# Reordered edges of a two-layer graph kernel: the weights' product, the first two pairs of scores, the last sums and the first block of layer 1

## The chip, the cores and the metric

The kernel runs on one NeuronCore of a Trainium2 chip. The metric is the device time of one execution in microseconds, as the median of several runs. The core has five engines that run side by side, each in its own program order: PE (TensorE, matrix products and transposes into the eight banks of PSUM), DVE (VectorE), ACT (ScalarE), POOL (GpSimd) and SP (SyncE, which here only issues DMAs). They wait for each other through semaphores.

## The reference

`x` is 4096 x 512 and `adj` 4096 x 4096 (mostly zeros). Two layers follow each other, each with a residual:

```python
# layer 0: attention with a dense bias
h = relu(layernorm(x))
q, k, v = h @ Wq.T + bq, h @ Wk.T + bk, h @ Wv.T + bv
a = q @ k.T / sqrt(512) + adj + adj
x = x + softmax(a) @ v
# layer 1: graph attention, 8 heads of 64
h = relu(layernorm(x))
nX = (h @ W) per head, standardized over its 64 values
kg = leaky_relu(at1 + at2.T, 0.2) * adj          # at1, at2: nX times a1, a2
x = x + elu(softmax(where(adj != 0, kg, -32768)) @ nX + nX)
```

## The kernel before

Rows are taken in 32 blocks of 128, eight superblocks ("sb") of four blocks, and eight chunks ("ic") of 512 query rows. Every helper call passes through `seq`, which keeps instructions in the order in which they are written, so the code's order is each engine's order.

**Weights.** The two weight matrices Wq and Wk are multiplied once, so that scores are h A h' with A = Wq' Wk. Each 128-row block of Wq and Wk is loaded (line 584, alternating), turned by four PE transposes into a bank and copied out by ACT (Wq) or DVE (Wk) (`turn_weights`, 590 to 594). After all eight come 16 products of 128 x 512 (line 607) with the contraction index in the outer loop and four banks `pa` open at once, and ACT moves the banks to `a_sb` (616).

**Projection.** For each superblock, `hidden(sb)` turns the normalized rows (PE 445, ACT relu 446) and POOL makes four sums `hS` of their blocks (454 to 457). `values_of(sb)` and `queries(sb)` are products in a form with seven instead of eight block products (`seven`, 491 to 517): four stages, PE products into banks Z and X, DVE additions out of them (512, 522, 556), and after each stage one function of the list `between`. `weight_sums` makes POOL's sums of the weights (470 to 473). The first superblocks have an order of their own: values 0, hidden 1, values 1, queries 0, hidden 2, queries 1; from superblock 2 on it is values, hidden of the next, queries. Stores of `qs`, `ts` to `q_d` (574) go through SP.

**Attention of layer 0.** A "pair" is two blocks of 128 keys against a chunk of 512 queries; 8 x 16 pairs, numbered by s = 0, 2, ..., 254. `stage(s, n)` for n = 0 to 3 makes the scores of a pair (line 724) in two halves of the bank `xz`, and DVE adds each part onto the turned block of `adj` (736); ACT takes the exponent (740). POOL makes the sums `S` of the pair (`pair_sums`, 752 to 764), and `weighted(s, ...)` adds the pair's seven products with the values to the banks M1 to M7 (779). In the main loop (891) `weighted(s)` and `stage(s + 2)` alternate. Before the loop, the stages of pair 0 run alone (880 to 882), and between them DVE turns the blocks 2 and 3 of `adj` (`swap`, 341) and prepares their masks for layer 1 (`for_layer_1`, 714 and 716, stored by SP at 717 and 718). DVE turns blocks 0 and 1 inside the last `queries` (681).

**Ends of chunks.** `chunk_end` (814) combines M1 to M7 into the output rows in pieces that `end()` issues. For the last chunk, `total_of_rows` (860) lets PE sum POOL's `total` over the partitions (867) before `weighted(254, (3, .), (6, .))`, and the last additions read bank M6 on DVE (835).

**Layer 1's projection.** A new set of pools is opened, among them a new PSUM pool over the same banks. `turn(r)` (1272) transposes the normalized block r (1275), ACT takes the relu (1276), `project(r)` multiplies it with W (1285), and `variance`, `deviation`, `standardize` follow. Block 0 is turned first, then block 1, then block 0 is projected. The main loop of layer 1 (512 steps, 1493) follows and isn't touched.

## Time and profile before

| | us |
|---|---|
| runs of the kernel: 3552.49, 3554.74, 3554.75 | median 3554.74 |
| the execution that was profiled | 3555.78 |
| its span in the profile | 3553.7 |
| PE busy | 3500.3 (98%) |
| DVE busy | 2572.2 (72%) |
| POOL busy | 2284.5 (64%) |
| ACT busy | 1770.7 (50%) |

The span is the time from the first to the last instruction of the profile; 2.1 us of the profiled execution lie outside of it. "Busy" counts a PE instruction from its start to its modelled end. An fp32 product of 128 x 128 by 256 columns is recorded as two matmul instructions. The program has three parts: the projection of layer 0 until 236 us, its attention until 1803 us, layer 1 from then on.

### The profile page before, as it was taken

Reading aid. Unit: us, or ns where it says so; the run is one execution under the profiler, and the core shown is the slowest. Engines: PE = TensorE matmul, PEld = TensorE weight load, DVE = VectorE, ACT = ScalarE, POOL = GpSimd, SP = SyncE. Lnnn points to the kernel's source line nnn. Section 1 sums busy time; section 2 is a strip of 40 time slices with the busy share of each in tenths; the row PEclk is TensorE's granted clock in tenths of the full one; section 3 lists DMA queues with packets and bytes.
Section 4 is the critical chain, followed back from the end, with each engine's and each line's share of the span. In section 5 each row is a group of like instructions: output and inputs, shape, how many; then the busy total and the mean of one; then the engine's idle time right before and its main releaser. Section 6 shows DMA issues by size and latency. Waiting matters only on the chain.

```text
span 3553.7 us, 59795 instructions
## 1 busy us (share of the span) xinstructions
PE 3500.3 (98%) x21898; PEld 2153.7 (61%) x21898; DVE 2572.2 (72%) x4256; ACT 1770.7 (50%) x1578; POOL 2284.5 (64%) x1863
## 2 busy tenths in 40 slices
PE   9999999999999999999999999999999999999998
PEld 7888888888888888888877222222322223222222
DVE  6765565656566666656557888888888888888887
ACT  2100111111111111111133899999999999999997
POOL 6754444444445444444556788888888888888886
PEclk9999999999999999999999999999999999999999
DMA  6678788888888888888758777777787777777775
GB/s 215 218 245 232 227 243 247 237 244 241 243 241 243 237 249 237 239 251 231 230 127 174 208 206 201 211 209 210 214 220 208 215 211 206 200 212 209 214 211 149
DMA packets 633358, 778.81 MB, mean 219 GB/s; under 512 B 78496, under 2 KB 461152, under 8 KB 623840
## 3 DMA queue, kind: packets, MB, share of 16 engines
q1 hardware_dynamic: 615344, 741.81, 72.4%
q0 software_dynamic: 16464, 31.98, 5.2%
q8 instruction: 174, 2.85, 0.3%
q10 hardware_dynamic: 1248, 1.11, 0.1%
q14 instruction: 128, 1.05, 0.1%
HBM read 592.71 MB, written 174.19 MB: 216 GB/s over the span
## 4 chain that ended last, share of the span: by engine, by line
PE 90%; DVE 7%; ACT 1%; DMA 1%; issue 1%; POOL 0%; SPq 0%; DVEq 0%; ACTq 0%; POOLq 0%
PE accs L1092 25%; PE XZ L724 21%; PE M L779 21%; PE r L1053 4%; PE r L1023 4%; PE l L1033 3%; PE X L505 3%; PE l L1053 3%; PE Z L505 2%; DVE t L1080 2%; PE y L1285 1%; PE pt L1156 1%; DVE x L835 1%; DVE y L1169 1%; PE accs L1285 1%
## 5 line engine op out<-in xcount | busy, mean ns | idle before, releaser
L1077 POOL TENSOR_TENSOR t<-t,g 128x1024 f32<-128x1024 f32 x512 | 1224.7, 2400 | 273.0 <-DVE t L1071 237.1
L1092 PE MATMUL accs<-t,nX 128*64 128x512 f32 x4096 | 1002.9, 605 | 4.7 <-DVE ob L1146 4.7
L1084 ACT ACTIVATE t<-t 128x2048 f32<-128x2048 f32 (+1 forms) x527 | 976.5, 1853 | 0.2 <-POOL t L1077 0.2
L1071 DVE SCALAR_TENSOR_TENSOR t<-u,at2m,r 128x512 f32<-128x512 f32 x1024 | 719.2, 744 | 193.6 <-issue 152.1
L740 ACT ACTIVATE aT<-aT 128x512 f32<-128x512 f32 x256 | 161.2, 630 | 1393.1 <-DVE aT L736 1393.1
L736 DVE TENSOR_TENSOR aT<-aT,XZ 128x256 f32<-128x256 f32 x891 | 351.5, 418 | 581.0 <-PE XZ L724 576.6
L1080 DVE TENSOR_TENSOR t<-l,g 128x1024 f32<-128x1024 f32 x512 | 623.6, 1218 | 0.0
L1039 ACT ACTIVATE l<-l 128x1024 f32<-128x1024 f32 x512 | 516.3, 1008 | 117.2 <-PE l L1033 66.0
L1092 PEld LDWEIGHTS accs<-t,nX 128*64 128x64 f32 x4096 | 246.5, 136 | 462.3 <-issue 449.6
L724 PE MATMUL XZ<-qt,hS 128*128 128x256 f32 x2040 | 483.0, 379 | 1.0
L752 POOL TENSOR_TENSOR S<-aT 128x256 f32<-128x256 f32 x128 | 93.2, 728 | 511.7 <-ACT aT L740 507.3
L724 PEld LDWEIGHTS XZ<-qt,hS 128*128 128x128 f32 x2040 | 386.8, 190 | 56.4 <-DVE aT L736 4.2
L724 PE MATMUL XZ<-qt,hT 128*128 128x256 f32 x1532 | 374.0, 380 | 3.7 <-DVE aT L736 3.7
L764 POOL TENSOR_TENSOR total<-total,aT 128x256 f32<-128x256 f32 x360 | 324.1, 914 | 9.4
L724 PEld LDWEIGHTS XZ<-qt,hT 128*128 128x128 f32 x1532 | 292.0, 191 | 44.1 <-DVE aT L736 4.1
L1023 PEld LDWEIGHTS <-z 6*128 6x128 bf16 x2048 | 52.4, 91 | 422.3 <-DVE t L1071 354.6
L753 POOL TENSOR_TENSOR aT<-aT 128x256 f32<-128x256 f32 x128 | 93.2, 728 | 285.7 <-ACT aT L740 285.7
L779 PE MATMUL M<-v,aT 128*128 128x256 f32 x1024 | 263.7, 380 | 0.0
L779 PE MATMUL M<-tv,aT 128*128 128x256 f32 x1024 | 262.6, 379 | 0.0
L779 PE MATMUL M<-v,S 128*128 128x256 f32 x1024 | 243.7, 381 | 0.0
L716 DVE SCALAR_TENSOR_TENSOR gs<-ng,aT 128x512 f32<-128x512 bf16 x254 | 224.5, 884 | 8.7
L779 PEld LDWEIGHTS M<-v,aT 128*128 128x128 f32 x1024 | 195.1, 191 | 26.7
(256 smaller groups left out, 4537.7 us busy)
## 6 DMA issues: line engine op xcount, KB each, us to landing
g<-gT_d SPq DMA_DIRECT2D x128, 1024.0 KB
ag<-in_adj_dram SPq DMA_DIRECT2D x256, 256.0 KB
hS<-s_d SPq DMA_DIRECT2D x64, 1024.0 KB
gT_d<-gs SPq DMA_DIRECT2D x256, 256.0 KB
nb<-nT_d SPq DMA_DIRECT2D x128, 512.0 KB
nx<-nT_d SPq DMA_DIRECT2D x256, 256.0 KB
hT<-h_d SPq DMA_DIRECT2D x64, 768.0 KB
tv<-vt_d SPq DMA_DIRECT2D x128, 384.0 KB
```

Source lines behind the costliest of these rows:

```text
L716: seq(nc.vector.scalar_tensor_tensor(gs, ng, G_MASKED / NEG_BIG, aT, ALU.mult, ALU.add))
L724: seq(nc.tensor.matmul(out, a, b, start=start and k == 0, stop=k == 1, skip_group_check=not start,))
L736: seq(nc.vector.tensor_add(p, before, part))
L764: seq(nc.gpsimd.tensor_add(t, t, a))
L779: seq(nc.tensor.matmul(sums[ic][i][:, u, :], a[:, ts(u, P)], b, start=jt == 0 and u == 0, stop=jt == NB - 2, skip_group_check=u == 1,))
L1039: seq(nc.scalar.activation(lefts[n], lefts[n], AF.Relu, scale=4.0))
L1053: seq(nc.tensor.matmul(out[first + 2 * r][ts(c, HD), :], ident_b[rows, rows], masks[r != c][rows, jt % JB, :], start=False, stop=True, ski ...
L1071: seq(nc.vector.scalar_tensor_tensor(t[:, 2 + e, :], u4[:, e, :], at2m[:, jt, h : h + 1], right[e], ALU.max, ALU.add))
L1077: seq(nc.gpsimd.tensor_mul(t[:, 2:4, :], t[:, 2:4, :], both_heads(n)))
L1080: seq(nc.vector.tensor_mul(logits[n][:, 0:2, :], lefts.pop(n), both_heads(n)))
L1084: seq(nc.scalar.activation(t, t, AF.Exp))
L1092: seq(nc.tensor.matmul(accs[ts(e, HD), hf, :], nX[jt // SB][:, jt % SB, hg * HG + 2 * hf + e, :], t[:, hf + 2 * e, :], start=jt == 0, stop ...
```

## The change

- The loads of Wk come before those of Wq. PE turns the four blocks of Wk and two of Wq, then makes the product for one output block (four products into one bank), turns the third block of Wq, makes the next output block, and so on; ACT and DVE take turns at the copies. `stats(0)`, `roots(0)`, `scale(0)` stand between the third and the fourth output block. bq is loaded by SP ahead of the second superblock of x, no longer by ACT.
- All superblocks run in the order values, hidden of the next, queries. The bias of the keys (`c_sb`) is made in four parts between the stages of values 0, the attention vectors between those of values 1; the loads of W move behind the load of superblock 3. `qs` is always the one buffer of its pool. `first_turned` takes the place of the buffer `prod`.
- DVE turns four blocks of `adj` inside the last `queries`. Before the main loop the stages of pairs 0 and 2 alternate, each pair with banks of its own; the masks of blocks 0 to 3 come later, one in each of four passes of the loop. The first pass has no scores to make, and its `weighted` has another order.
- In the last chunk the sums of M6 are copied by ACT to `of_6`, from which DVE adds them. `total_of_rows` of the last chunk comes after the last products, and its result is copied to SBUF by DVE. Block 0 of layer 1 is loaded in the last chunk (`load_first`) and turned in its last pass (`turn_first`) through the bank `xz` into `first_turned`; layer 1's loop turns block 1 before it projects block 0.

```diff
-            for k in range(KC):
-                for name, w in (("q", wqT), ("k", wkT)):
+            for name, w in (("k", wkT), ("q", wqT)):
+                for k in range(KC):
                     seq(nc.sync.dma_start(out=raw[name][:, k, :], in_=w[ts(k, P), :]))
...
+            seq(nc.sync.dma_start(out=bq_sb, in_=bq[None, :].to_broadcast([P, D])))
             xts[1] = load_x(1)
...
             for k in range(KC):
-                turn_weights("q", k, nc.scalar.copy)
-                turn_weights("k", k, nc.vector.tensor_copy)
-            for c in range(SB):
-                for k in range(KC):
+                turn_weights("k", k, nc.vector.tensor_copy if k % 2 else nc.scalar.copy)
+            for k in range(2):
+                turn_weights("q", k, nc.vector.tensor_copy if k % 2 else nc.scalar.copy)
+            for k in range(KC):
+                pa = psum.tile([P, 512], F32, name="pa", tag="XZ"[k % 2], bufs=2)
+                for c in range(SB):
                     seq(nc.tensor.matmul(
-                        pa[k], turned["q"][:, c, ts(k, P)], turned["k"][:, c, :],
+                        pa, turned["q"][:, c, ts(k, P)], turned["k"][:, c, :],
                         start=c == 0, stop=c == SB - 1,
                     ))
-            stats(0, *range(SB))
-            roots(0)
-            scale(0)
+                if k + 2 < KC:
+                    turn_weights("q", k + 2, nc.scalar.copy)
+                elif k + 1 < KC:
+                    stats(0, *range(SB))
+                    roots(0)
+                    scale(0)
+                seq(nc.scalar.activation(a_sb[:, k, :], pa, AF.Identity, scale=half_scale))
             stats(1, *range(SB))
...
             hidden(0, xts.pop(0))
+            wa = weight_sums(a_sb, [t.rearrange("p (k c) -> p k c", k=2) for t in ats])
             scale(1)
...
+            def key_bias(k):
+                w = wk_rows[:, k, :]
+                seq(nc.vector.tensor_mul(w, w, bq_sb))
+                seq(nc.vector.tensor_reduce(c_sb[:, k : k + 1], w, AX.X, ALU.add))
+                if k + 1 == KC:
+                    seq(nc.vector.tensor_scalar_mul(c_sb, c_sb, half_scale))
...
-            queries(0, [lambda: next(vectors, None)] * 4)
-            hidden(2, xts.pop(2))
-            queries(1, ahead_of(3))
-            for sb in range(2, NS):
+            for sb in range(NS):
                 if sb + 2 < NS:
                     xts[sb + 2] = load_x(sb + 2)
...
-                    firsts = [t.rearrange("p h e -> p (h e)") for t in aa]
+                    firsts = [t.rearrange("p h e -> p (h e)") for t in aa] + [bv_sb, ats[0]]
                     queries(sb, [
-                        lambda s=s: turn_blocks(firsts[s], raws.pop(s), s) for s in range(2)
+                        lambda s=s: turn_blocks(firsts[s], raws.pop(s), s) for s in range(SB)
                     ])
...
-            w = {"alone": psum.tile([P, 2, H], F32, name="z0", tag="M3", bufs=1)[:, 0]}
-            for n, (f, s) in enumerate(((swap, 2), (for_layer_1, 2), (swap, 3), (for_layer_1, 3))):
-                stage(0, n, w)
-                f(s)
+            both = [
+                (0, {"alone": True, "z": bank_of(3), "x": bank_of(6)}),
+                (2, {"alone": True, "z": bank_of(5), "x": xz[:, 1]}),
+            ]
+            for n in range(4):
+                for s, w in both:
+                    stage(s, n, w)
+            w = {}
             pair_sums(0)
-            for s in range(2):
+            pair_sums(2)
+            for s in range(4):
                 later.setdefault(2 * s, []).append(lambda s=s: for_layer_1(s))
...
-                more, ahead = s + 2 < n_tiles, s + 4 < n_tiles
+                more, ahead = 0 < s < n_tiles - 2, s + 4 < n_tiles
...
+                if s == 0:
+                    weighted(0, (1, 0), (1, 1), (2, 0), (2, 1), (4, 0), (4, 1), (7, 0), (7, 1))
+                else:
+                    weighted(s, (1, 0), (1, 1), (7, 0))
...
-                if not more:
+                if s + 2 == n_tiles:
+                    turn_first()
+                if s + 2 == n_tiles:
+                    end()
+                weighted(s, (3, 0), (3, 1), (6, 0), (6, 1))
+                if s + 2 == n_tiles:
                     end()
                     total_of_rows(ic)
-                weighted(s, (3, 0), (3, 1), (6, 0), (6, 1))
...
-                    then((add, c12, c12, m[3]), (add, c12, c12, m[6]),
-                         (add, c21, c21, m[6]), (add, c22, c22, m[6])),
+                    then((add, c12, c12, m[3]), (copy, of_6, m[6])),
+                    then((add, c12, c12, of_6), (add, c21, c21, of_6), (add, c22, c22, of_6)),
...
+                if ic + 1 == NI:
+                    totals_sb = prep.tile([P, SB], F32, name="totals_sb")
+                    seq(nc.vector.tensor_copy(totals_sb, pt4))
+                    pt4 = totals_sb
...
+            def turn_first():
+                for k in range(KC):
+                    seq(nc.tensor.transpose(
+                        xz.rearrange("p u h -> p (u h)")[:, ts(k, P)], firsts[-1][:, ts(k, P)], ident
+                    ))
+                seq(nc.scalar.activation(
+                    first_turned, xz.rearrange("p u h -> p (u h)"), AF.Relu
+                ))
...
-        m = one_bank("r0" if r else "r1")
+        m = one_bank("r0")
...
-                    ys[r][:, g, 0:HW], h1s[:, r % 2, ts(k, P)], w1_sb[:, k, g, :],
+                    ys[r][:, g, 0:HW], (h1s[:, r % 2] if r else first_turned)[:, ts(k, P)], w1_sb[:, k, g, :],
...
-                turn(r + 1)
+                if r >= 0:
+                    turn(r + 1)
```

## The prediction

> **What bounds the kernel now.** I read the page's rows of busy time first, then PE's waits, then the time line at the places where it waits.

> ```profile
> PE 3500.3 (98%) x21898; PEld 2153.7 (61%) x21898; DVE 2572.2 (72%) x4256; ACT 1770.7 (50%) x1578; POOL 2284.5 (64%) x1863
> ...
> PE XZ L724 <- DVE aT L736: 3.7, 1, 3.7
> ...
> PE m L1275 <- issue: 2.1, 1, 2.1
> ...
> PE Z L505 <- POOL hS L454: 0.9, 1, 0.9
> PE XZ L867 <- POOL total L764: 0.9, 1, 0.9
> PE pa L607 <- DVE v L594: 0.8, 1, 0.8
> ```

> PE is busy in 98% of the span, and the table of waits (total, times, longest) shows few and single ones. So a change can only gain where PE stands still, or where it runs slowly after standing still. The granted clock shows the second (columns: window; length; busy time of PE, PEld, DVE, ACT, POOL; clock; DMA share; GB/s):

> ```profile
> 243.00:244.00 1.00, 0.00 (x0) 0.00 (x0) 0.09 (x1) 0.00 (x0) 0.00 (x0) 1.00 1.07 345
> ...
> 247.00:248.00 1.00, 1.00 (x4) 0.81 (x3) 0.11 (x1) 0.00 (x0) 0.00 (x0) 0.50 0.01 4
> ...
> 1798.00:1799.00 1.00, 0.17 (x1) 0.00 (x0) 0.75 (x3) 0.00 (x0) 0.92 (x3) 1.00 0.00 0
> 1799.00:1800.00 1.00, 0.87 (x7) 0.79 (x7) 0.56 (x1) 0.00 (x0) 0.68 (x1) 1.00 0.00 0
> ...
> 1801.00:1802.00 1.00, 1.00 (x4) 0.82 (x3) 0.34 (x1) 0.00 (x0) 0.00 (x0) 0.50 0.00 0
> ...
> 1810.00:1811.00 1.00, 1.00 (x3) 0.72 (x3) 0.00 (x0) 0.00 (x0) 0.00 (x0) 0.50 0.00 0
> ```

> After two pauses of PE the clock is 0.50 for 7 and for 10 us: four matmuls in a microsecond instead of some six. The change touches both places.

> **1. Weights' product.** Before, the product starts at 11.27 (0.78 after the last transpose ended, waiting for a copy) and ends at 25.11: 13.84 us. Afterwards it needs six turned blocks instead of eight. In the trace the fifth block's copy (ACT) runs from 8.73 to 9.32 and the sixth block's transposes end about 9.2; the order of the blocks in the queue changes, not their number or size, so these are the times of the first Wq block and of the second. Start 9.4. The two blocks that are left cost 4 x 0.109 us each inside the product (16 transposes of `hidden` take 1.74 us): 0.87. End 9.4 + 13.84 + 0.87 = 24.1: **gain 1.0**. What must not be late: `scale(0)`. The statistics follow their data (before, to 14.4), POOL's roots take 3.1, so it can start by 17.6 and takes 2.9, and the transposes that need it start at 24.1. On ACT it stands ahead of the third and fourth copies to `a_sb`, whose products end at about 20.6 and 24.1. bq's load goes ahead of superblock 1's rows: 256 KB at about 390 GB/s is 0.7 us later, needed much later.

> **2. One order.** Removed: before values 1, PE waits 0.95 + 0.22 us for POOL's `hS` (46.66 and 48.02) and 0.35 for the relu (41.94). POOL is late there because `tv` sums stretch to 2.8 us next to DVE's 2.3 us multiplication and because `hS` is needed at once. Afterwards queries 0 (12.1 us of PE) stand between `hidden(1)` and values 1. POOL's queue then: `hS`(0) to about 32.0, the weights' sums (4 x 1.27) to 37.1, eight `tv` sums to 43.5, `hS`(1) to 48.6; PE needs it from 56. The keys' bias moves between the stages of values 0: per stage 4 additions x 0.42 plus about 1.3 on DVE, 3.0 of the 3.46 us that PE takes; no cover lost, but with POOL beside it an operation can stretch (1.43 in the trace), then the two banks per half give one stage of room. SP: superblock 2 is loaded after `hS`(0), landing near 41, wanted at 43.7; superblock 3 after the stores of queries 0, near 62 to 67, wanted at 69.7. **Gain 1.5**; bounds 0 (a late load holds DVE's queue, the additions stand behind it) and 1.9.

> **3. First two pairs.**

> ```profile
> 241.01 1.03 PE L724 MATMUL XZ<-qt,hS 128*128 128x256 f32 x4
> ...
> 243.91 0.43 DVE L714 TENSOR_SCALAR ng<-aT 128x512 bf16<-128x512 f32 x1 [3.14 <-DMA q_d<-qs]
> ...
> 245.78 2.07 PE L724 MATMUL XZ<-qt,hT 128*128 128x256 f32 x4 [3.75 <-DVE aT L736]
> 247.65 1.91 PE L779 MATMUL M<-v,aT 128*128 128x256 f32 x4
> ...
> 261.51 1.03 PE L779 MATMUL M<-v,aT 128*128 128x256 f32 x4
> ```

> DVE stands 3.14 us at the first mask `ng`, whose memory is given free by the last store of `qs`; the additions that PE waits for are behind it in DVE's queue. Then PE runs at half clock until 251.2. Pair 0's own products start at 236.59, pair 2's first weighted product (all of pair 0 and pair 2's scores done) at 261.51. The same work without a pause: a stage 0, 1 or 2 is 8 instructions x 0.216 = 1.73, stage 3 is 0.87, so two pairs take 2 x 6.05 = 12.1; `weighted(0)` is 28 x 0.216 = 6.05. 236.59 + 18.15 = 254.7: **gain 6.8**. What is late next: the exponent of block 1 is ready 0.6 us before its products' turn at 249.6; POOL's S3 at about 246, needed at 251.3; `tv`, loaded at 242.6 before and as early now, needed at 250.4. The masks moved behind these stages: DVE turns and masks blocks 4 and 5 and masks block 0 from 249.3 on, about 5.4 us with a wait for the two mask buffers' stores; its next score is due at 257. The 0.58 wait of the first product for the last `qs` stays: it looks like a wait for the old banks as a whole. If it went too, 7.3.

> **4. End of layer 0.** Before, from the end of product (5, 1) at 1798.01: a pause of 0.88 and 0.16 for POOL's total (done 1799.69), the sums over partitions to 1800.2, M3 and M6 in 3.1 instead of 1.73, a pause of 2.1, transposes of two blocks 1.94, and block 0's projection until 1813.02.

> ```profile
> 1803.36 1.88 DVE L835 TENSOR_TENSOR x<-x,M 128x512 f32<-128x512 f32 x3 [1.02 <-PE M L779]
> ...
> 1805.45 1.94 PE m L1275 x8
> ...
> L1275 PEldq EVENT_SEMAPHORE  x2: 51/2666/5280, 1800.0 to 1805.3; - x2
> ```

> The third row names what "issue" hides: PE's sequencer holds a semaphore wait from 1800.0 to 1805.3, that is, until DVE's last addition out of M6 (to 1805.24). Afterwards: block 0's transposes 0.44 (to 1798.45), M3 and M6 1.73 (1800.18, POOL's total is there), sums over partitions 1.0 (1801.2), then a pause for DVE's small copy, about 0.45, ACT's copy of M6 (0.57) being done by 1801.0; block 1's transposes and block 0's projection at full clock 4.0 (the pitch of later blocks): 1805.65. Gain 7.3. DVE's three additions now follow in 2.1 us beside the projection; the relu of block 1 needs the pool's memory that they free, near 1804.3, and its product starts at 1806.1: cover 1.2 us.

> [...] But the trace throttled at 1800.9 after idle time of only 1.04 us plus 1.1 us of one-column sums, and not after single pauses of 0.78 (10.49) and 0.74 (235.85). The new stretch, sums 1.0 plus pause 0.45, is about 1.5, between 0.8 and 2.1, nearer the one that throttled. The low clock would last about the half of its 6.8 us at 244.4 to 251.2, since no pause follows: 3.4 us at half speed, 1.7 lost. I take the row: **gain 5.6**, ends 4.0 (6.8 us slow) and 7.3.

> **Sum.** 1.0 + 1.5 + 6.8 + 5.6 = 14.9. Profiled: span 3553.7 to 3538.8, with the 2.1 outside 3540.9. The median of the runs is 1.0 below the profiled execution: **3539.8**.

> **Rivals.**
> (a) The wait in front of pair 0 changes its name: DVE, POOL or a load is late by a step I have not seen, PE pauses again near 250 and the clock falls. For it: three engines and SP change order there; against: each lead above is 0.6 us or more. With half of gain 3 lost and 1 and 2 at their low ends: 3554.7 - (3.4 + 0.5 + 5.6) = 3545.
> (b) Layer 1's start still waits for the last additions (the new bank counts as the old one until 1804.2). For it: PE's first product of the attention waited for the last reader of all old banks. Against: no addition reads a bank any more. Gain 4 falls to about 2.5 (2.5 us pause, slow clock): 3543.
> (c) The change doesn't mend the start: product and order gain nothing, hidden by data: 3542.3.
> (d) Slower. Layer 1 runs 512 steps at 2.966 us of PE, and ACT has 1.01 + 1.90 = 2.91 in each. If the new layout of tiles stretched ACT by more than 0.06, ACT would set the step; it decides from 0.03 us a step on (15 us in all); at 0.06 us it gives 3540 + 31 = 3571. For it: this thin margin. Against: nothing in these steps is edited.

> **Chances.** Forecast (3536 to 3542) 0.68, (a) 0.12, (b) 0.07, (c) 0.07, (d) 0.03, a mixture of (a) to (c) that leaves under 7 us 0.03. The range 3535 to 3546 takes in the forecast with all bounds and most of (a) to (c). A measurement can tell about 0.2% (7 us) from no change: faster 0.91, same 0.05, slower 0.04.

> **What would show it.** Right: the weights' product from about 9.4 to 24.1; no PE wait on `hS`; no PE wait over 1 us in the first 25 us of the attention, and no clock of 0.50 there; after the attention a PE pause under 0.6 us and at most 3.4 us of low clock. Wrong: a new row among PE's waits in these three places, or a pitch of layer 1 other than 2.966.

## The result and the profile after

| | before | after |
|---|---|---|
| median of the runs, us | 3551.82 (3549.65 to 3554.75, 6 runs) | 3538.76 (3537.04 to 3540.84, 6 runs) |
| ratio | | 0.9962, 95% interval 0.9949 to 0.9975 |
| the execution that was profiled, us | 3555.78 | 3538.39 |
| its span, us | 3553.7 | 3536.6 |

The change makes the kernel faster by 13.1 us (0.38%) in the medians, and by 17.1 us between the two profiled executions. The forecast was 3539.8. The difference between 13.1 and 17.1 matters below: over all six runs, the execution of before on which the prediction was built turned out to lie 4.0 us above the median, not 1.0.

The row of busy times on the page of the new kernel, to be set beside 3500.3 us of PE before:

```profile
PE 3492.0 (99%) x21898; PEld 2149.6 (61%) x21898; DVE 2574.3 (73%) x4262; ACT 1771.1 (50%) x1580; POOL 2285.6 (65%) x1863
```

Its table of PE's waits (total, times, longest):

```profile
PE M L777 <- DMA tv<-vt_d: 0.8, 1, 0.8
...
PE of L722 <- DVE qs L557: 0.6, 1, 0.6
...
PE Z L508 <- ACT hT L449: 0.4, 1, 0.4
PE m L1317 <- issue: 0.4, 1, 0.4
```

The rows for `aT` (3.7), `issue` (2.1), `hS` (0.9), `total` (0.9) and `v` (0.8) are gone or are down to 0.4. One wait is new: 0.8 us for a load of `tv`, once, at 301 us; no other profile below has it there. The number of matmul records is the same and PE is busy 8.3 us less, mostly because before some of them ran at a granted clock of 0.50: PE was busy in 13.5 us of the two low stretches, so by about 6.8 us too long. The time line of PE at the three places (start, length, what ran, idle time ahead of it):

```profile
9.33 3.70 PE L610 MATMUL pa<-v 128*128 128x512 f32 x8
...
24.04 1.91 PE L448 MATMUL pt<-ident,xt 128*128 128x128 f32 x16
...
233.22 2.86 PE L722 MATMUL of<-qt,hT 128*128 128x256 f32 x12 [0.58 <-DVE qs L557]
...
251.45 1.03 PE L777 MATMUL M<-v,aT 128*128 128x256 f32 x4
...
1787.13 1.89 PE L777 MATMUL M<-tv,aT 128*128 128x256 f32 x8
1788.85 0.60 PE L890 MATMUL XZ<-ident,xn 128*128 128x128 f32 x4
1789.29 1.89 PE L777 MATMUL M<-v,S 128*128 128x256 f32 x8
1791.02 0.95 PE L869 MATMUL XZ<-ones,total 128*128 128x1 f32 x8
1792.34 0.63 PE L1317 MATMUL m<-ident,xns 128*128 128x128 f32 x4 [0.37 <-issue]
1792.80 3.73 PE L1327 MATMUL y<-w_sb,first_turned 128*128 128x264 f32 x16
1796.36 0.60 PE L1317 MATMUL m<-ident,xns 128*128 128x128 f32 x4
```

And the windows at the two places that ran at a clock of 0.50 before (window; length; busy time of PE, PEld, DVE, ACT, POOL; granted clock; DMA share; GB/s):

```profile
247.00:248.00 1.00, 1.00 (x7) 0.87 (x6) 0.97 (x2) 0.00 (x0) 0.92 (x2) 1.00 0.41 172
...
1791.00:1792.00 1.00, 0.97 (x9) 0.86 (x7) 0.04 (x1) 0.58 (x1) 0.00 (x0) 1.00 0.00 0
1792.00:1793.00 1.00, 0.66 (x5) 0.69 (x6) 0.89 (x5) 0.00 (x0) 0.00 (x0) 1.00 0.00 0
```

Seven matmuls in a microsecond where there were four, and 1.00 right through. The end of layer 0 is counted here and below from the end of product (5, 1), the last row of products ahead of the end, to the first transposes after block 0's projection: 1789.02 (1787.13 + 1.89) to 1796.36. Before, the same stretch runs from 1798.17 (1796.28 + 1.89) to 1812.86.

The spans of the two profiled executions, cut at the same places of the work:

| stretch | before | after | difference |
|---|---|---|---|
| start to the transposes of `hidden(0)` | 25.11 | 24.04 | -1.07 |
| to those of `hidden(2)` | 42.87 | 40.64 | -2.23 |
| to pair 0's first product | 168.61 | 168.54 | -0.07 |
| to pair 2's first weighted product | 24.92 | 18.23 | -6.69 |
| to the end of (5, 1) of the last pair | 1536.66 | 1537.57 | +0.91 |
| end of layer 0 | 14.69 | 7.34 | -7.35 |
| layer 1 | 1740.84 | 1740.24 | -0.60 |
| sum | | | -17.10 |

### The profile page after: what moved, and what is told of

Its sections match the earlier page's. It is cut to its first block, busy times and chain, and to the rows that moved or that the text cites. A ratio compares the mean times of both kernels' runs of the same rounds, so it can differ in the third digit from the quotient of the medians.

```text
span 3536.6 us, 59808 instructions
## 1 busy us (share of the span) xinstructions
PE 3492.0 (99%) x21898; PEld 2149.6 (61%) x21898; DVE 2574.3 (73%) x4262; ACT 1771.1 (50%) x1580; POOL 2285.6 (65%) x1863
## 4 chain that ended last, share of the span: by engine, by line
PE 90%; DVE 7%; ACT 1%; DMA 1%; issue 1%; SPq 0%; DVEq 0%; ACTq 0%
PE accs L1134 25%; PE XZ L722 21%; PE M L777 20%; PE r L1095 4%; PE r L1065 4%; PE l L1075 3%; PE X L508 3%; PE l L1095 3%; PE Z L508 2%; DVE t L1122 2%; PE y L1327 1%; PE pt L1198 1%; DVE x L837 1%; DVE y L1211 1%; PE accs L1327 1%
## 5 line engine op out<-in xcount | busy, mean ns | idle before, releaser
L714 DVE SCALAR_TENSOR_TENSOR gs<-ng,aT 128x512 f32<-128x512 bf16 x252 | 222.7, 884 | 8.7
```

The source lines that it names most:

```text
L714: seq(nc.vector.scalar_tensor_tensor(gs, ng, G_MASKED / NEG_BIG, aT, ALU.mult, ALU.add))
```

## The experiments

Three questions: does each part bring what its stretch shows; what exactly removed the pauses; and what lets the clock fall. All edits are to the new kernel unless said otherwise ("-" is the new kernel).

### Each part undone alone

**u_pairs** puts the old start of the attention back:

```diff
-            for n in range(4):
-                for s, w in both:
-                    stage(s, n, w)
+            w = {"alone": psum.tile([P, 2, H], F32, name="z0", tag="M3", bufs=1)[:, 0]}
+            for n, (f, s) in enumerate(((swap, 2), (for_layer_1, 2), (swap, 3), (for_layer_1, 3))):
+                stage(0, n, w)
+                f(s)
```

> The changed kernel with the old start of the attention (pair 0 alone, blocks 2 and 3 of adj turned and masked between its stages). Theory (each part gains at its own place and nothing later takes it back): about 6.7 us longer than the changed kernel, the pause of 3.7 us and a clock of 0.50 back after 236 us, no other place changed: 3545.5. Rival (the gain of one place is partly absorbed by a wait further on): the same pause at its place, but the end only 2 to 4 us later.

**u_end** puts the old end back: M6 read by DVE, the sums over partitions ahead of the last products, block 0 turned in layer 1.

```diff
-                    then((add, c12, c12, m[3]), (copy, of_6, m[6])),
-                    then((add, c12, c12, of_6), (add, c21, c21, of_6), (add, c22, c22, of_6)),
+                    then((add, c12, c12, m[3]), (add, c12, c12, m[6]),
+                         (add, c21, c21, m[6]), (add, c22, c22, m[6])),
...
-                    turn_first()
```

> The changed kernel with the old end of layer 0 (sums over partitions before the products with M3 and M6, DVE adds straight out of M6, block 0 turned in layer 1). Theory: pauses of about 1.0 and 2.1 us before layer 1 and a low clock after them are back, 5 to 8 us longer than the changed kernel by where the clock falls: 3544 to 3547. Rival (layer 1's projection has waits of its own that hide part of it): less than 4 us.

**u_weights** has the old product of the weights (eight turned blocks first):

```diff
-                turn_weights("k", k, nc.vector.tensor_copy if k % 2 else nc.scalar.copy)
-            for k in range(2):
-                turn_weights("q", k, nc.vector.tensor_copy if k % 2 else nc.scalar.copy)
+                turn_weights("q", k, nc.scalar.copy)
+                turn_weights("k", k, nc.vector.tensor_copy)
```

> The changed kernel with the old order of the weights' loads, transposes and products. Theory: the first transposes of hidden start at about 25.1 instead of 24.05, and all later work with them: 1.1 us longer, 3539.9. Rival (the start is hidden behind the loads or by the order of the superblocks): no difference at superblock 2, 0.0 us.

**u_order** has the old order of the first superblocks:

```diff
+            values_of(0, None)
+            hidden(1, xts.pop(1))
...
+            queries(0, [lambda: next(vectors, None)] * 4)
+            hidden(2, xts.pop(2))
+            queries(1, ahead_of(3))
-            for sb in range(NS):
+            for sb in range(2, NS):
```

> The changed kernel with the old order of superblocks 0 to 2 and the keys' bias in one piece. Theory: the pauses before the values of superblock 1 are back, and their true cost is what the starts of the instructions show, 2.2 us (the idle column shows 1.5): superblock 2's transposes start 2.2 us later, 3541.0. Rival (the idle column is the cost): 1.5 us.

| kernel | median, us | over the new kernel's 3538.76 | its stretch | the same in the new kernel |
|---|---|---|---|---|
| u_weights | 3539.84 (5 runs) | +1.1 | 25.71 | 24.04 |
| u_order | 3542.08 (8) | +3.3 | 42.87 | 40.64 |
| u_pairs | 3542.42 (7) | +3.7 | 21.53 | 18.23 |
| u_end | 3544.38 (11) | +5.6 | 13.01 | 7.34 |

The ratios to before (0.9963, 0.9968, 0.9973 and 0.9977) carry intervals of about plus or minus 0.0012, some 4 us. The four were also timed in another session than the new kernel, in which the kernel before had a median of 3552.97 us and not 3551.82. The differences in the table add up to 13.7, beside 13.1 for the whole change; set against the kernel before of their own session they are -0.1, 2.2, 2.5 and 4.5, and add up to 9.1. So the medians do not tell whether the parts help or hinder each other, and the split rests on the stretches.

The totals of u_weights and u_end came as expected; u_order's lay 1.1 us over the expected 3541.0. For the weights, though, the stretch does not settle the size either: the start of `hidden(0)` also moves with the landing of the first weights. In nine profiles with the new product it lay between 23.52 and 26.37 us, in the three with the old one (before, before_again, u_weights) at 25.11, 24.64 and 25.71. What the profiles do show is that the old product waits 0.78 us for a copy in each of the three, and the new one at most 0.24.

u_order settles which of two readings of the trace counts. The idle column had promised 1.5 us; the starts said 2.2. PE's waits in u_order have the old rows back:

```profile
PE Z L508 <- POOL hS L457: 0.9, 1, 0.9
...
PE X L508 <- POOL hS L458: 0.2, 1, 0.2
```

and yet its stretch is longer by 2.23, exactly as between before and after. A start is recorded, an end is modelled; each of the three pauses, counted from a modelled end, came out some 0.2 us short here (1.52 us in all, where the starts give 2.23).

u_pairs missed: 6.7 was expected and 3.3 (stretch) or 3.7 (median) came. Its time line:

```profile
240.15 1.13 PE L722 MATMUL XZ<-qt,hT 128*128 128x256 f32 x4 [2.01 <-DVE aT L734]
```

The pause is 2.01 us instead of 3.75, and the clock stayed at 1.00. To learn whether that lies in the kernel or in the execution, both were profiled once more.

> The kernel before, profiled a second time. Theory (the length of the pause inside pair 0 is the time that the last store of queries needs to land, which differs from execution to execution, and whether the clock falls after it is a matter of where it lies on the grid): the same wait of the first mask for the store, between 1 and 3.2 us, and PE's pause as much longer than the store's landing as before; low clock possible at both places, in multiples of 3.41 us. Rival (the pause belongs to the kernel): 3.7 to 3.8 us again, and 7 us of low clock.

> u_pairs, profiled a second time. Theory (landing time differs from execution to execution): PE's pause inside pair 0 is not 2.0 again but anywhere from 1.5 to 3.8, and from pair 0's first product to pair 2's first weighted product 21 us or more. Rival (the other order of the queries halved the wait): 2.0 again within 0.2 us, and 21.5 with clock 1.00.

The kernel before, second profile, time line of PE and DVE:

```profile
241.79 0.43 DVE L714 TENSOR_SCALAR ng<-aT 128x512 bf16<-128x512 f32 x1 [1.51 <-DMA q_d<-qs]
...
243.66 2.07 PE L724 MATMUL XZ<-qt,hT 128*128 128x256 f32 x4 [2.11 <-DVE aT L736]
...
1801.08 1.06 PE L1275 MATMUL m<-ident,xns 128*128 128x128 f32 x8 [2.13 <-issue]
```

Same chain, other sizes. The mask waits for the same store, but this time the store was free 2.6 us after its issue (239.17 to 241.79) and not 4.2 us (239.67 to 243.91). The pause is 2.11 us, with one stretch of 3.4 us at a clock of 0.50 behind it; the whole stretch is 22.24 us instead of 24.92. At the end of layer 0 the same pauses (0.89 and 2.13 us) cost no low clock at all: 11.25 us instead of 14.69. In u_pairs_again the pause was 2.02 us and the stretch 21.28, so the expectation that it would spread evenly over 1.5 to 3.8 was a miss: three of four profiles show 2.0 to 2.1, and the first one of before, on which the prediction was built, is the exception. In the trace of that store fifteen of its sixteen parts had landed by 242.07 and the last at 243.78; why that one was late the runs do not show.

### What removed the pauses

**one_pair** keeps the masks out of the way (they stay in the loop), but runs pair 0's stages alone:

```diff
-                for s, w in both:
-                    stage(s, n, w)
+                stage(0, n, w)
...
-                more, ahead = 0 < s < n_tiles - 2, s + 4 < n_tiles
+                more, ahead = s + 2 < n_tiles, s + 4 < n_tiles
```

> The new kernel, but before the loop only pair 0's stages run, without pair 2's between them; the masks stay in the loop and four blocks of adj are turned early. Theory (the pause came from the masks in DVE's queue, which waited for a store): PE's pauses inside pair 0's stages add up to 1.0 us or less, and from pair 0's first product to pair 2's first weighted product it takes 18.5 to 19.5 us; total 3539 to 3540.5. Rival (one pair alone is too little work to cover DVE's additions and the exponent, so it is pair 2's stages in between that remove the pause): pauses of 2 us or more, stretch 20.5 to 21.5 or more, total 3541 to 3543.

Median 3542.87 us (6 runs). Time line of PE, then windows:

```profile
239.09 1.13 PE L722 MATMUL XZ<-qt,hT 128*128 128x256 f32 x4 [0.51 <-DVE aT L734]
240.06 1.03 PE L777 MATMUL M<-v,aT 128*128 128x256 f32 x4
243.12 0.67 PE L777 MATMUL M<-tv,S 128*128 128x256 f32 x2 [2.03 <-POOL S L752]
```

```profile
243.00:244.00 1.00, 0.88 (x4) 0.83 (x5) 0.00 (x0) 0.00 (x0) 0.92 (x3) 1.00 1.07 444
...
245.00:246.00 1.00, 1.00 (x4) 0.82 (x3) 0.00 (x0) 0.00 (x0) 0.00 (x0) 0.50 0.96 405
```

Each theory was half right. Without the masks the pause for DVE shrinks to 0.51 us, so the masks were its cause. But a wait of 2.03 us takes its place, and the clock falls after it. The view names POOL's sums `S` for it, as the third of them (line 752) ended just ahead. That name does not hold. The product that waits is number 7 of pair 0. It reads the first of the sums (line 750, done at 239.70) and `tv`. Here are one_pair's load of `tv`, and then two lines of u_pairs, where the same product starts before the third sum does and the view names the load:

```profile
238.62 0.42 SPq L694 DMA_DIRECT2D tv<-vt_d  x1
```

```profile
242.93 0.67 PE L777 MATMUL M<-tv,S 128*128 128x256 f32 x2 [0.78 <-DMA tv<-vt_d]
243.47 0.73 POOL L752 TENSOR_TENSOR S<-aT 128x256 f32<-128x256 f32 x1
```

In one_pair the load was issued behind the stores of the queries, and its last part landed at 242.99, 0.1 us ahead of PE. So two waits lay one behind the other, for DVE and then for the load of `tv`. Together they are 2.54 us in one_pair and 2.79 in u_pairs: moving the masks alone would have gained next to nothing (the stretch is 22.98 us, 233.13 to 256.11, with a fall of the clock in it; 21.53 and 21.28 in u_pairs' two profiles without one). In the new kernel this load lands no earlier, at 243.05, but PE wants it only at 247.13: the stages of pair 2 are what covers it.

**m6_direct** lets DVE read bank M6 again and changes nothing else of the end:

```diff
-                    then((add, c12, c12, m[3]), (copy, of_6, m[6])),
-                    then((add, c12, c12, of_6), (add, c21, c21, of_6), (add, c22, c22, of_6)),
+                    then((add, c12, c12, m[3])),
+                    then((add, c12, c12, m[6]), (add, c21, c21, m[6]), (add, c22, c22, m[6])),
```

> The new kernel without of_6: DVE's last additions read bank M6 itself again; the sums over partitions stay last and block 0 stays turned early. Theory (the pause before layer 1 came from the new pool waiting for DVE's last reading of a bank): PE waits about 2.0 to 2.5 us, recorded as issue, ahead of the transposes of block 1, and the end of layer 0 takes 9.5 us instead of 7.5, or up to 12 if the clock falls; total 3541 to 3543.5. Rival (of_6 is not needed once the sums are last, as the additions are early enough): pause under 0.8 us, total within 1 us of 3538.8.

Median 3542.12 us (6 runs). Time line of PE and DVE, then windows:

```profile
1791.40 0.95 PE L865 MATMUL XZ<-ones,total 128*128 128x1 f32 x8
...
1792.87 1.88 DVE L833 TENSOR_TENSOR x<-x,M 128x512 f32<-128x512 f32 x3
...
1794.85 1.09 PE L1313 MATMUL m<-ident,xns 128*128 128x128 f32 x4 [2.50 <-issue]
```

```profile
1794.00:1795.00 1.00, 0.15 (x1) 0.18 (x2) 1.00 (x3) 0.00 (x0) 0.00 (x0) 0.50 1.03 311
...
1796.00:1797.00 1.00, 1.00 (x3) 0.74 (x3) 0.00 (x0) 0.60 (x1) 0.00 (x0) 0.50 1.05 246
```

"issue" again stands for DVE's last three additions, which run to 1794.75; PE starts 0.1 us later. The clock falls inside the pause and stays at 0.50 for 6.8 us, and the end takes 12.28 us. The theory holds, a little over its upper end of 12: without ACT's copy of M6, the late sums and the early turn of block 0 leave a longer pause than before (2.50 against 2.13), as the additions now come after the small operations on the sums.

**sums_early** puts only the sums over partitions back ahead of the last products:

```diff
+                    total_of_rows(ic)
                 weighted(s, (3, 0), (3, 1), (6, 0), (6, 1))
                 if s + 2 == n_tiles:
                     end()
-                    total_of_rows(ic)
```

> The new kernel, but the sums over partitions come before the products (3, .) and (6, .) again, with ACT's copy of M6 and the early turn of block 0 kept. Theory (each wait counts by its length only): PE waits about 0.5 us for POOL's total, then about 0.9 us for ACT's copy of M6 before block 1 is turned: end of layer 0 8.4 to 9.0 us instead of 7.5, clock 1.00, total 3539.5 to 3540.5. Rival (sums of one column next to a pause drop the clock, as in the kernel before): 0.50 shows within 3 us behind the sums for 3.4 us or more, end of layer 0 10 us or more, total 3541.5 to 3543.

Median 3540.46 us (5 runs). Time line of PE:

```profile
1790.29 1.02 PE L869 MATMUL XZ<-ones,total 128*128 128x1 f32 x8 [0.78 <-ACT first_turned L893]
1791.17 1.97 PE L777 MATMUL M<-v,S 128*128 128x256 f32 x8
1793.82 0.66 PE L1317 MATMUL m<-ident,xns 128*128 128x128 f32 x4 [0.68 <-ACT of L837]
```

The end takes 8.80 us with the clock at 1.00 throughout, 1.5 us more than in the new kernel: two pauses and nothing else. The name of the first one is another than expected, ACT's relu out of the bank that the sums are to use. So ACT's copy of M6 is most of part 4 (4.9 of 5.7 us by the stretches, low clock included), and the place of the sums is worth 1.5 us. The early turn of block 0 was not undone alone.

### What lets the clock fall

The prediction had taken 1.7 us off part 4 for a low clock that did not come: sums of 0.95 us and a pause of 0.37 (0.72 in one_pair) were not enough in any of the six profiles with this end (after, u_pairs, u_pairs_again, u_weights, u_order, one_pair). **doses** measures what is enough. It adds 47 doses to the attention loop, of two kinds in five lengths each:

```diff
+                if s >= 8 and s % 4 == 0 and 4 <= s % NB < NB - 4:
+                    dose(*doses[(s // 4) % len(doses)])
```

> The new kernel with 47 added doses inside the attention of layer 0, one in every second pair, in a cycle of ten: 6, 10, 14, 18 or 22 one-column products in a row (about 1.4 to 5.2 us by 0.24 us each), and pauses of PE in which ACT runs 0, 2, 4, 6 or 8 operations in a chain between two one-column products (about 1 to 4 us). They change no output. Theory A (for the clock, one-column products count as idle time): the clock falls to 0.50 after most doses of one-column products that last over 2 us, as often as after pauses of the same length. Theory B (they count as work): it never falls after one-column products of any length, and only after pauses, from about 2.5 us on always and between 1 and 2.5 us sometimes. Total 137 us of doses without low clock: 3675; with low clock of 3.4 us or more after 20 to 30 doses 40 to 80 more.

It took 3766.4 us (one run), with 157 us of low clock, which cost up to half of that; the total came out 11 us above the upper end, as the pauses were longer than thought (0.5 to 5.4 us). Two doses of the same length, ten one-column products each, in the time line of PE, and the windows behind each:

```profile
541.66 2.29 PE L931 MATMUL XZ<-ones,ident 128*128 128x1 f32 x20
...
825.81 2.29 PE L931 MATMUL XZ<-ones,ident 128*128 128x1 f32 x20
```

```profile
543.82:547.00 3.18, 3.18 (x17) 2.82 (x17) 1.14 (x3) 0.00 (x0) 2.98 (x5) 1.00 0.85 328
828.00:829.00 1.00, 1.00 (x6) 0.90 (x7) 0.00 (x0) 0.00 (x0) 1.00 (x2) 1.00 0.92 362
829.00:830.00 1.00, 1.00 (x4) 0.78 (x3) 0.00 (x0) 0.00 (x0) 0.92 (x2) 0.52 1.23 424
...
832.00:833.00 1.00, 1.00 (x5) 0.83 (x5) 0.93 (x3) 0.00 (x0) 0.00 (x0) 0.77 0.96 386
```

The first left the clock alone. After the second it fell at 829.04 and rose at 832.46, 3.42 us later. Both were full stretches of PE by the column of busy time. So theory B is out: ten one-column products, 2.29 us without a pause, brought the clock to 0.50 as idle time did. But theory A, which asks for a length only, does not tell these two doses apart either.

The clock's changes, read from windows of 0.5 us, do. There were 30 falls and 30 rises between 293 and 1979 us, and all 60 lie within 0.04 us of one grid of 3.413 us that runs through all of it; every low stretch is 3.41, 6.83 or 10.24 us long, one, two or three steps. The first dose began 2.75 us after a line of the grid, so that no window held more than about 1.6 us of it; the second began 0.2 us after a line and lay in one window whole. If one adds up for each window of the grid the pauses and the one-column products in it, all 30 falls came after windows with 2.20 us or more, every window with 2.11 or less left it alone, and none lay between. Six one-column products in a row never brought a fall, ten did in two of five doses, fourteen in three of six, 18 and 22 in all ten. Pauses of 0.5 to 1.1 us never did; those of 1.6 us, with a one-column product at either end, did in two of three, one of 2.2 us did, those of 2.6 us did in two of three, and longer ones always.

**doses2** puts this to the test with pauses each of which is too short alone:

```diff
+            def dose(between):
+                hold()
+                if between:
+                    for e in range(between):
+                        seq(nc.tensor.matmul(xz[:, 1, 0:P], ident, wide, start=True, stop=True))
+                    hold()
```

> The new kernel with 47 doses that change no output, in turn: one pause of PE; two such pauses with 0.43 us of full products between them; two with 3.5 us of full products between them. One pause is about 1 us and 1.5 us with the one-column products at its ends. Theory (the clock goes by the share of a window of 3.41 us on a fixed grid in which PE has no full products, and falls where that is over 2.1 us): never after one pause, never after two that are 3.5 us apart, and after those that are 0.43 us apart in more than half of the cases, all changes on one grid of 3.41 us. Rival (the longest single pause decides, and where the grid lies does not): none of the three falls, as no pause is over 1.5 us, or all two-pause doses behave alike.

Two doses of the near kind, with equal pauses, in the time line of PE, and the windows behind the first:

```profile
759.66 0.28 PE L930 MATMUL XZ<-ones,ident 128*128 128x1 f32 x2
760.84 0.38 PE L934 MATMUL XZ<-spare,ident 128*128 128x1 f32 x2 [0.91 <-ACT spare L933]
...
762.80 0.38 PE L934 MATMUL XZ<-spare,ident 128*128 128x1 f32 x2 [0.91 <-ACT spare L933]
...
846.65 0.28 PE L930 MATMUL XZ<-ones,ident 128*128 128x1 f32 x2
...
849.79 0.38 PE L934 MATMUL XZ<-spare,ident 128*128 128x1 f32 x2 [0.91 <-ACT spare L933]
```

```profile
763.00:764.00 1.00, 1.00 (x6) 0.92 (x6) 0.00 (x0) 0.00 (x0) 0.92 (x3) 0.93 1.11 377
764.00:765.00 1.00, 1.00 (x4) 0.74 (x4) 0.00 (x0) 0.00 (x0) 0.85 (x2) 0.50 0.91 354
```

The first dose brought a fall at 763.85, the second none. Over the run: single pauses 0 falls in 16, near pairs 6 in 15, far pairs 1 in 16. Near pairs fell less often than the "more than half" that was expected, and the one far pair that fell began with a pause of 1.5 us, some 2.0 with the products at its ends, just at the limit. All 14 changes lie within 0.01 us of a grid of 3.413 us. In this run six of the seven falls came after windows with 2.35 us or more and one after 2.16; five windows with 2.15 to 2.17 and all with less brought none. So the limit lies at about 2.1 to 2.2 us in both runs. The rival, the longest single pause, falls: equal doses differ by where they lie.

Last, **m6_fill** gives PE work in the pause of m6_direct:

```diff
                     end()
                     total_of_rows(ic)
+                    for e in range(5):
+                        seq(nc.tensor.matmul(
+                            xz[:, 1], ident, firsts[-1][:, 0:H], start=True, stop=True
+                        ))
```

> m6_direct with five products of 128 x 128 by 256 columns (2.16 us, results unused) behind the sums over partitions, where PE waited 2.5 us. Theory (the low clock comes from PE without full products, whatever it waits for): the clock stays 1.00 there, the end of layer 0 takes 9.4 to 9.9 us instead of 12.4, total 2.5 to 3 us under m6_direct: 3539 to 3540.5 by the median. Rival (the wait itself costs all, the products only add work): 0.50 still shows, total 3542 or more.

```profile
1791.41 2.42 PE L968 MATMUL XZ<-xn,ident 128*128 128x256 f32 x10 [0.32 <-DVE totals_sb L871]
1793.90 0.66 PE L1317 MATMUL m<-ident,xns 128*128 128x128 f32 x4
1794.39 3.73 PE L1327 MATMUL y<-w_sb,first_turned 128*128 128x264 f32 x16
```

In the time line of PE the clock stays at 1.00 there (block 0's projection takes 3.73 us, in m6_direct 6.12), and the end takes 9.81 us instead of 12.28: as expected, and block 1 no longer waits for DVE's additions. The total missed: 3541.77 us (7 runs), 0.35 under m6_direct instead of 2.5 to 3, and not even that when each is set against the kernel before of its own session (3552.10 and 3553.98). In this profile the clock fell at 1824.9 instead, for 3.4 us early in layer 1, where the new kernel and m6_direct have the same wait but no fall (see the last section); how often m6_direct falls in the executions that were not profiled is not known. So filling the pause works where it is done, and that it makes the kernel faster is not shown.

No variant is clearly faster than the new kernel; sums_early is 13.5 us faster than the kernel before of its session, the new kernel 13.1, too close to tell. What is left of pauses at the places of the change is 0.58, 0.4 and 0.37 us and once 0.8.

## Why the prediction was right

**What bounds.** Right: PE stayed the bound, and the pauses that went are the gain.

**1. Weights' product.** Start 9.33 for 9.4, end 24.04 for 24.1, gain 1.07 for 1.0; undone alone, 1.1. That the sizes agree so well is in part luck, as the landing of the first weights moves this stretch by more than the gain; the wait that was to go (0.78) did go.

**2. One order.** The mechanism held, no wait for `hS` is left, and no load came late. The size was off: 2.23 instead of 1.5, over the upper bound of 1.9. The step that failed is reading the gain from the idle column, whose pauses begin at modelled ends. Starts at both sides of the stretch give the right number.

**3. First two pairs.** 18.23 us for 18.15, clock at 1.00, and the 0.58 wait stayed as said. Gain 6.69 for 6.8 against this execution of before. Two things were not seen. The sum took the late store and the two low windows of one execution as the kernel's own; undone alone, the part is worth 3.3 by its stretch and 3.7 by the median. And the text names the masks alone as what holds PE. one_pair shows a second wait of 2.0 us, for the load of `tv`, right behind it, which pair 2's stages cover. The list of what is late next had `tv` and found it in time, because it looked at the new order only.

**4. End of layer 0.** Gain 7.35 for 5.6: the term of 1.7 us for a low clock was wrong, the rest (7.3) right within 0.1. The row was read too simply. In before, 1.04 us of idle time and 1.1 us of one-column sums lay in one window of the grid (2.17 us by the same count, the clock fell at its end). before_again has the same row without a fall: a line of the grid cuts it, and its windows hold 1.70 and 1.58 us. The new end has 0.95 + 0.37 = 1.3, and no position can bring that to the 2.1 to 2.2 us of the dose runs. "Nearer the one that throttled" interpolated where the first dose run shows a step: no fall up to 2.11 us in a window, a fall from 2.20 on.

**Sum.** The forecast took 14.9 and 1.0 off the profiled execution of before, 15.9 in all; the median after lies 17.0 below it (3555.78 less 3538.76). Of these 17.0, however, 4.0 are that execution's own distance from the median of before, and 13.1 the change's gain in medians. So the parts were worth less on the median than the sum of 14.9, while against this one execution they were worth more, and the time came out within 1.0 us partly by cancellation. What made the execution dear: the falls of the clock took 2.7 us at pair 0 (half of the 5.4 us that PE was busy in them) and about 3.4 at the end of layer 0 (beside before_again), the late store 1.6. Other executions have some of this, too.

**Rivals.** (a) did not come; its kind is what one_pair met. (b) did not: the wait ahead of block 1 was 0.37, and m6_direct shows what it would have been (2.50). (c) did not, and (d) did not: layer 1 took 1740.24 us, 0.60 less than before. Not foreseen was the wait of 0.8 us for a load of `tv` at 301 us, most of the 0.91 us lost inside the attention. It stands in none of the other profiles with this loop, so it is of this execution; no run here tried what made that load late.

## What to carry to other kernels

Where a wait is to be removed, ask what PE would wait for next in the old order, not only in the new one: here two waits lay behind each other, and only the change that covers both gained. Doubt the name that a view gives to a wait when another run shows the same instruction going ahead without it. Read a gain from the starts of instructions at both sides of a stretch, and profile the kernel twice before a sum is made against one execution: the same pauses at the end of layer 0 cost 3.4 us more in one execution than in the other. When a pause can't go, set it against what was measured here: apart from the fall at the very end of this text, the smallest windows of 3.41 us ahead of a fall held 2.02 us of pauses and one-column products.

## What the runs showed of the hardware

The same twelve profiles hold a test that nobody set up. Early in layer 1, which the change leaves as it is, PE waits 2.12 us for DVE in each of them, as here in the new kernel and in m6_fill:

```profile
1823.31 2.05 PE L1327 MATMUL accs<-w_sb,h1s 128*128 128x264 f32 x8 [2.12 <-DVE at L1371]
```

```profile
1824.90 3.73 PE L1327 MATMUL accs<-w_sb,h1s 128*128 128x264 f32 x8 [2.12 <-DVE at L1371]
```

In five of them (before_again, u_pairs, u_end, one_pair, m6_fill) the wait lies whole in one window of the grid, and the clock falls; in the other seven a line of the grid cuts it, no window there holds more than 1.84 us, and it does not.

Whether this wait of 2.12 us brought a fall thus went with where the execution lay on the grid. At the granted 0.50, a fall costs by estimate half of the time that PE is busy in it, so up to 1.7 us for each 3.41 us that it lasts. Layer 1 took 1741.8 to 1742.6 us in u_pairs, u_end, one_pair and m6_fill, and 1740.2 to 1740.9 in the seven without that fall (1745.7 in before_again, where another follows at 1895.6). How much of the spread between the runs that were not profiled comes from this is not shown.

One fall does not fit the count. In all twelve profiles the clock also falls once between 1937 and 1955 us and stays low for 17.07 us, the longest low stretch of all. In eleven of them the window ahead of it holds only 1.3 to 1.8 us of pauses. PE runs products of 6 and of 64 rows there; no run tried how those count.
